# A segment attention kernel on one core: GpSimd's fills issued a segment later, the fourth segment's owners computed one step sooner, another PSUM bank for the last prefix, and one table's work placed behind a row's scaling

## The chip, the cores and the metric

The kernel runs on one core of a Trainium2 chip. The metric is the device time of one execution in microseconds (us); the number given for a kernel is the median of several executions. The engines are written as in the profile: PE is TensorE, DVE is VectorE, ACT is ScalarE, POOL is GpSimd, SP is SyncE, which here only starts transfers. PEld is the weight load of PE.

## The reference

16384 tokens with 256 features each carry a segment number from 0 to 7. Attention runs inside each segment, and a column normalisation over all tokens follows. The segment numbers are not sorted, so that `searchsorted` gives a start for each segment, and a token's position is its distance to that start; positions outside 0 to 3071 wrap or are dropped by the scatter. The part that matters:

```python
q = feat @ Wq; k = feat @ Wk; v = feat @ Wv              # 256 -> 32, 32, 256
starts = jnp.searchsorted(bids, jnp.arange(B, dtype=bids.dtype))
pos = jnp.arange(N, dtype=bids.dtype) - starts[bids]
pad = lambda x: jnp.zeros((B, LMAX, x.shape[-1]), x.dtype).at[bids, pos].set(x)
mask = jnp.zeros((B, LMAX), bool).at[bids, pos].set(True)
scores = jnp.einsum('bld,bmd->blm', pad(q), pad(k))
attn = jax.nn.softmax(jnp.where(mask[:, None, :], scores, NEG), axis=-1)
t = jnp.einsum('blm,bmd->bld', attn, pad(v))[bids, pos] @ Wt
tn = (t - t.mean(0)) / jnp.sqrt(t.var(0) + EPS) * gamma + beta
return feat + jax.nn.relu(tn)
```

## The kernel before, in words

Every engine has its own instruction stream, and the order inside a stream is the order in which the Python code emits the operations. `pg.op` records what each operation reads and writes, and puts a semaphore wait in front of it wherever it needs something of another engine. So a line that is moved in the Python code is moved in its engine's queue, with everything that it issues, and an operation that has to wait holds back all that stands behind it on its engine.

**Stages.** A setup reads the segment numbers, searches the starts, and prepares segments 0 and 1. Then a loop over segments e = 0 to 6 works in steps u = 0 to 5, written (e,u) here. In it segment e is attended, segment n = e+1 is projected and scored, and the rows of segment e+2 are listed and gathered. Segment 7 and the normalisation follow, with the stores of all rows.

**A segment** has up to six tiles of 128 rows; tiles 4 and 5 are guarded by a run-time count (`present`), and segments 0 and 1 have four tiles with this input. A conditional operation passes its semaphore to the next unconditional one of its engine.

**Listing.** For each segment, DVE's `owners(e)` (seven operations) marks the tokens that own a slot and ends with a running count in `lm[:, e]`. `prefix(lo, hi, bank)` adds the counts over partitions with two small PE products into a PSUM bank; DVE reads it as `cbeg`, `n_bc` and `n_1`. `list_tests` makes two comparison masks `ge` of 128x768 on DVE (fp16 in, bf16 out, line 835), `list_half(e, h, bank)` multiplies them on PE (six products) and its `finish` turns the result into row numbers `idx` on DVE (`lr`, `junk`, `jc`, `idx`) and issues three gathers `xs<-in_r_feat,idx` on POOL.

**Attending.** `attend(e,u)` is a row of products `ps<-vs,pa` on PE into bank 4 or 5 by the parity of u. `attended(e,u)` takes a reciprocal `rdens` on DVE (line 859) and scales the row on ACT into `tk` (line 817). Only then may attend(e,u+2) write the bank again. `xt_main` and `xt_rest` transpose gathered rows into `xT`, `project` makes q and k (`k` is copied by DVE, `q` by ACT), `scores` makes `pa`, `values` makes `vs`.

**PSUM banks.** Banks 0 to 3 are `ps_s`, 4 and 5 `ps_o`, 6 and 7 `ps_m`. `nb()` hands out banks 6 and 7 in turn to `xt_main`, `xt_rest`, `project` and `values`.

**Fillers.** `everyone()` and `tables()` are lists of small DVE jobs for all segments at once. `slot()` takes the next one off the list `work`; the table `steps` says at which steps of e = 0 to 3 one is taken. In e = 0 the jobs of u = 1 to 5 are a, b, `third`, c, d; in e = 1 those of u = 0, 1, 2, 4, 5 are f, g, h, g2, and the first of `tables()` (`frow`, `gbase`, `w`). `third` handles segment 3: `owners(3)`, its prefix and its `list_tests`. Job g is the prefix of segments 4 to 8, h makes `reads` from `br_f`, g2 reads the table `turn_of`.

**Fills.** POOL sets several tensors to constants: `acc` (the sums of the normalisation, 128x512), `xl` and `tl` (128x768), `ridl`, `ecat` (128x512) and sixteen single elements of `turn_of`. `moments` adds into `acc` on DVE from (1,1) on.

Of the kernel before, what the change touches and what calls it, by code (L numbers as in the profile page):

```python
# [899 lines left out]
def fast_path(nc, feat, bids, wq, wk, wv, wt, gamma, beta, out, bad):  # L900
# [231 lines left out]
    pg.set("POOL", ones_n[:], 1.0 / N)  # L1132
    pg.set("POOL", rdens[:], 1.0)
    pg.set("POOL", graw[:], 0.0)
    for i in range(4):
        s = slice(32 * i, 32 * i + NB)
        pg.dma("SP", graw[s, 0, :], gamma.rearrange("(c i) -> c i", i=32))
        pg.dma("SP", graw[s, 1, :], beta.rearrange("(c i) -> c i", i=32))
# [311 lines left out]
    xt_rest(0, sB)  # L1450
    h1()
    last_()
    pg.set("POOL", acc[:], 0.0)
    pg.set("POOL", xl[:], 0.0)
    pg.set("POOL", tl[:], 0.0)
    pg.set("POOL", ridl[:], NB * FW)
    pg.set("POOL", ecat[:], 0.0)
    for i, g in enumerate(ORDER):
        pg.set("POOL", turn_of[:, g : g + 1], float(i + 1))
    values(0, 0, bank[1])  # L1460
    scores(0, 0, range(4))
    project(0, 1, ps_m[0])
# [22 lines left out]
    def everyone():  # L1485
# [24 lines left out]
            pg.scan(lm[:, NB, 0:J], ones[:], lose[:])  # L1510

        def g():
            for go in prefix(4, NL, ps_s[3]):
                go()

        def g2():
# [161 lines left out]
    reads_at = {(NB - 4, 2 + t): (NB - 2, (t,)) for t in range(4)}  # L1678
    reads_at.update({(NB - 3, t): (NB - 2, (3 + t,)) for t in (1, 2)})
    reads_at.update({(NB - 3, 3 + t): (NB - 1, (2 * t, 2 * t + 1)) for t in range(3)})  # L1680
    lag, ready = [], []
    steps = {0: (1, 2, 3, 4, 5), 1: (0, 1, 2, 4, 5), 2: (0, 2, 3, 5), 3: (0, 1, 2, 3, 5)}
    def third():
        owners(3)
        first, then, last_ = prefix(3, 4, ps_s[3])
        first()
        then()
        last_()
        list_tests(3, FT)
# [3 lines left out]
    for e in range(NB - 1):  # L1693
# [11 lines left out]
        for u in range(FT):  # L1705
            if ahead <= NB and u == 0 and e:
                first = list_half(ahead, 0, ps_s[2])
            attend(e, u)
            if e == 0 and u == 0:
                second_list()  # L1710
                attended(e, u)
                first = list_half(ahead, 0, ps_s[2])
            if ahead <= NB and u == 0:
                first()
                if LTs == FT:
                    second = list_half(ahead, 1, ps_s[3])
            slot(int(u in steps.get(e, range(FT))))
            if u == 4 and e + 3 <= NB and e:
                list_tests(e + 3, FT if e + 3 < NB else LT)
            if u == 4:  # L1720
                values(n, 0)
            if u == 5:
                values(n, 1)
            if e == NB - 2 and u == 3:
                group_in(1)
            if (e, u) != (0, 0):
                opened = attended(e, u)
            if u == 0:
                if ahead <= NB and LTs == FT:
                    second()  # L1730
                if ahead == NB:
                    others()
                xt_main(n, 0)
                xt_main(n, 1)
            if u == 1:
                xt_rest(n)
                project(n, 0)
                scores(e, 1, None)
            if u == 3:
                project(n, 1)  # L1740
                scores(n, 0, range(4))
            if u == 4:
                scores(n, 0, range(4, 6))
            if u == 5:
                values(n, 2)
            for x in ready:
                moments(*x)
            ready = []
            lag.append((e, u))
            for _ in range(0 if e == 0 else 2 if u % 2 else 1):  # L1750
                if lag:
                    square(*lag[0])
                    ready.append(lag.pop(0))
            if e == 0 and u == 1:
                pg.tr32(gb[:].rearrange("p s i -> p (s i)"), graw[:].rearrange("p s i -> p (s i)"))
                for e_ in range(3, NB):
                    pg.dma(
                        "SP", xs[:, e_ * FT : (e_ + 1) * FT, :], zt[:].unsqueeze(1).to_broadcast([P, FT, D]), [opened]
                    )
            if e == 0 and u in (1, 5):  # L1760
                pg.copy("ACT", spot[:], ones[:, 0:1])
            if (e, u) in reads_at:
                gather_reads(*reads_at[e, u], opened)
            if e == NB - 2 and u == 1:
                group_in(0)
            if e == NB - 2 and u > 3:
                group_in(u - 2)
            if e == NB - 2 and u == 5:
                group_in(4)
            if e == 4 and u == 3:  # L1770
                pg.set("POOL", tk[:, TT - 2 : TT, :], 0.0)
                pg.register("POOL", "writes", writes[:], 16 * (6 * NB + LT), 16 * (4 * NB + LT - 1))
                pg.register("POOL", "lastg", lastg[:], NG, 1)
                pg.register("POOL", "third", third_l[:], 1)
                for e_ in range(NB):
                    pg.register("POOL", ("g", e_), upto[0:1, e_ : e_ + 1], NG, 1)
                    pg.register("POOL", e_, tiles_i[0:1, e_ : e_ + 1], 2)
# [238 lines left out]
```

## Time and profile before

| | |
|---|---|
| time, median of 3 runs | 312.52 us (310.84 to 314.01) |
| the profiled execution's own time | 313.69 us |
| its span, first to last instruction | 311.4 us |
| PE busy | 252.2 us, 81% |
| DVE busy | 229.3 us, 74% |
| ACT busy | 135.8 us, 44% |
| POOL busy | 129.7 us, 42% |
| mean granted TensorE clock | 0.906 |

A row of the timeline gives the start in us, the duration, the engine and line, the operation with what it writes and reads, how many were merged, and in brackets how long the engine stood idle before it and what ended that. A row of the stage view gives a stretch of time, its length, each engine's busy time, the granted clock (1.00 is full, 0.50 half), the share of the DMA engines and GB/s. Lines such as L807 or L835 are those of helpers, so that groups are told apart by the names of the tiles.

### The profile page before, as it was taken

The numbers are of one execution on the slowest core, as the hardware profiler recorded it, in microseconds if no ns is written. First come the engines' busy times: TensorE is split into PE (matmuls) and PEld (weight loads), VectorE is DVE, ScalarE is ACT, GpSimd is POOL, SyncE is SP. The second block draws the span as 40 slices with busy tenths as digits, with TensorE's granted clock in tenths as the row PEclk, the third lists the DMA queues.
The fourth block names the chain that finished last, engine by engine and source line by source line (L and its number), as shares of the span: only waits on it lengthen the run. The fifth ranks groups of instructions, "written<-read, shape, count | busy, mean of one in ns | idle before, by whom it ended". The sixth has DMA issues, their size and how long they took to land.

```text
span 311.4 us, 4481 instructions
## 1 busy us (share of the span) xinstructions
PE 252.2 (81%) x1194; PEld 166.8 (54%) x1194; DVE 229.3 (74%) x718; ACT 135.8 (44%) x292; POOL 129.7 (42%) x155
## 2 busy tenths in 40 slices
PE   1779689899799898999999999989977786573820
PEld 1656555766575677687878778757523221121200
DVE  7866788779999896736664765767389999999600
ACT  7346234258474628644754583564421121211110
POOL 3436580340350071006312853742212347778674
PEclk9989796999999999999999999999998579859575
DMA  3102069422122021112021320579999999999984
GB/s 98 35 24 67 3 203 346 157 82 69 52 84 71 34 70 29 67 61 80 27 95 36 90 94 24 196 259 378 339 364 408 349 421 413 402 419 393 424 358 177
DMA packets 23240, 56.82 MB, mean 182 GB/s; under 512 B 4768, under 2 KB 15858, under 8 KB 19114
## 3 DMA queue, kind: packets, MB, share of 16 engines
q1 hardware_dynamic: 17434, 45.77, 39.2%
q0 software_dynamic: 5232, 10.18, 10.2%
q10 hardware_dynamic: 544, 0.52, 0.5%
q8 instruction: 13, 0.21, 0.3%
q14 instruction: 17, 0.14, 0.1%
HBM read 26.73 MB, written 28.61 MB: 178 GB/s over the span
## 4 chain that ended last, share of the span: by engine, by line
PE 39%; DVE 30%; DMA 14%; ACT 7%; issue 6%; POOL 2%; DVEq 1%; SPq 0%; POOLq 0%; ACTq 0%
PE ps L807 37%; DMA out<-f 14%; DVE acc L846 4%; DVE f L826 3%; DVE w L826 2%; DVE junk L833 2%; PE ps L812 2%; DVE k L823 2%; DVE tk L826 2%; POOL out L892 2%; ACT pa L817 1%; DVE ge L835 1%; ACT xT L817 1%; ACT tk L817 1%; DVE both L851 1%
## 5 line engine op out<-in xcount | busy, mean ns | idle before, releaser
L882 POOL DMA_INDIRECT xs<-in_r_feat,idx x48 | 51.0, 1063 | 101.2 <-DVE idx L846 77.1
L807 PE MATMUL ps<-vs,pa 128*128 128x257 f32 x312 | 73.6, 384 | 4.7 <-ACT sq L817 3.6
L807 PEld LDWEIGHTS ps<-vs,pa 128*128 128x128 f32 x312 | 57.1, 189 | 16.5 <-ACT sq L817 4.8
L807 PE MATMUL ps<-f,ident 128*128 128x512 f32 x52 | 38.3, 855 | 19.6 <-DMA f<-in_r_feat 14.4
L892 POOL DMA_INDIRECT out<-tk,idx x39 | 42.9, 1100 | 26.8 <-DVE tk L826 10.4
L817 ACT ACTIVATE tk<-ps,rdens 128x256 f32<-128x256 f32 x46 | 22.2, 483 | 61.8 <-DVE rdens L859 61.8
L807 PE MATMUL ps<-wvt,xT 128*128 128x256 f32 x156 | 39.6, 405 | 0.3 <-ACT pa L817 0.3
L822 ACT COPY f<-ps 128x512 f32<-128x512 f32 x26 | 13.9, 590 | 58.9 <-PE ps L807 58.9
L807 PEld LDWEIGHTS ps<-wvt,xT 128*128 128x128 f32 x156 | 30.9, 202 | 11.0 <-issue 4.3
L807 PEld LDWEIGHTS ps<-f,ident 128*128 128x128 f32 x52 | 11.7, 259 | 36.5 <-DMA f<-in_r_feat 19.3
L846 DVE SCALAR_TENSOR_TENSOR acc<-sq,reads_r,acc 128x256 f32<-128x256 f32 x45 | 21.6, 480 | 8.8 <-ACT sq L817 8.8
L817 ACT ACTIVATE pa<-ps,mask 128x512 f32<-128x512 f32 x39 | 24.0, 690 | 7.5 <-PE ps L807 7.4
L826 DVE TENSOR_TENSOR tk<-tk,ps 128x1024 f32<-128x1024 f32 (+1 forms) x30 | 24.2, 843 | 0.3
L882 POOL DMA_INDIRECT reads_r<-reads_of,idx x12 | 13.4, 1120 | 24.8 <-ACT sq L817 11.8
L826 DVE TENSOR_TENSOR f<-f,ps 128x512 f32<-128x512 f32 x38 | 23.3, 681 | 0.6 <-PE ps L807 0.6
L807 PE MATMUL ps<-q,k 32*128 32x512 f32 (+2 forms) x154 | 21.2, 486 | 1.5 <-ACT pa L817 1.1
L846 DVE SCALAR_TENSOR_TENSOR acc<-tk,reads_r,acc 128x256 f32<-128x256 f32 x45 | 21.5, 478 | 1.2 <-ACT tk L817 0.7
L807 PE MATMUL ps<-xT,w 128*128 128x512 f32 (+1 forms) x60 | 20.5, 474 | 0.5 <-ACT xT L817 0.4
L823 DVE COPY k<-ps 32x128 f32<-32x128 f32 x40 | 11.8, 294 | 12.0 <-PE ps L807 11.1
L807 PE MATMUL ps<-vs,pb 128*128 128x257 f32 x82 | 19.6, 387 | 0.0
L807 PEld LDWEIGHTS ps<-vs,pb 128*128 128x128 f32 x82 | 15.0, 189 | 6.5 <-issue 2.3
L817 ACT ACTIVATE q<-ps,cqk 96x512 f32<-96x512 f32 (+3 forms) x24 | 14.6, 608 | 7.3 <-PE ps L807 7.0
(260 smaller groups left out, 357.1 us busy)
## 6 DMA issues: line engine op xcount, KB each, us to landing
f<-in_r_feat SPq DMA_DIRECT2D x16, 1024.0 KB, 12.8
out<-f SPq DMA_DIRECT2D x16, 1024.0 KB, 15.8
t_rows<-tk SPq DMA_DIRECT2D x8, 512.0 KB, 3.9
xs<-zt SPq DMA_DIRECT2D x5, 768.0 KB, 10.3
t_rows<-tk SPq DMA_DIRECT2D x8, 256.0 KB, 2.2
eb<-edge_of SPq DMA_DIRECT2D x16, 96.0 KB, 2.3
xs<-in_r_feat,idx POOLq DMA_INDIRECT x48, 2.8
out<-tk,idx POOLq DMA_INDIRECT x39, 7.2
```

The lines of the kernel that those rows point to most:

```text
L807: "PE", lambda e: e.matmul(out, lhsT, rhs, start=start, stop=stop, skip_group_check=True),
L812: return self.op("PE", lambda e: e.transpose(out, in_, ident), [in_, ident], [out])
L817: "ACT", lambda e: e.activation(out, in_, func, bias=bias, scale=scale), [in_, *more], [out]
L822: return self.op("ACT", lambda e: e.copy(out, in_), [in_], [out])
L823: return self.op(eng, lambda e: e.tensor_copy(out, in_), [in_], [out])
L826: return self.op(eng, lambda e: e.tensor_tensor(out, a, b, op), [a, b], [out])
L833: lambda e: e.tensor_scalar(out, a, s1, s2, op0, op1, accum_out=accum)
L835: else e.tensor_scalar(out, a, s1, s2, op0, op1),
L846: else e.scalar_tensor_tensor(out, a, s, b, op0, op1),
L851: return self.op("DVE", lambda e: e.tensor_reduce(out, in_, AX.X, op), [in_], [out])
L882: lambda e: e.indirect_dma_start(out=out, out_offset=None, in_=table, in_offset=bass.IndirectOffsetOnAxis(ap=ind, axis=0), bounds_check=n ...
L892: lambda e: e.indirect_dma_start(out=table, out_offset=bass.IndirectOffsetOnAxis(ap=ind, axis=0), in_=src, in_offset=None, bounds_check=n ...
```

## The change

Five edits. The fill of `acc` goes from the end of the setup to its beginning. The other fills go into `later_sets`, which is called at the end of (1,0). `owners(3)` leaves `third` and is emitted in (0,0), behind `attended(0,0)` and ahead of the list of segment 2. The prefix of segments 4 to 8 takes its bank from `nb()` instead of bank 3. At (1,5) the slot is taken behind `attended` instead of ahead of it.

```diff
     pg.set("POOL", graw[:], 0.0)
+    pg.set("POOL", acc[:], 0.0)
...
-    pg.set("POOL", acc[:], 0.0)
-    pg.set("POOL", xl[:], 0.0)
-    pg.set("POOL", tl[:], 0.0)
-    pg.set("POOL", ridl[:], NB * FW)
-    pg.set("POOL", ecat[:], 0.0)
-    for i, g in enumerate(ORDER):
-        pg.set("POOL", turn_of[:, g : g + 1], float(i + 1))
+
+    def later_sets():
+        pg.set("POOL", xl[:], 0.0)
+        pg.set("POOL", tl[:], 0.0)
+        pg.set("POOL", ridl[:], NB * FW)
+        pg.set("POOL", ecat[:], 0.0)
+        for i, g in enumerate(ORDER):
+            pg.set("POOL", turn_of[:, g : g + 1], float(i + 1))
+
...
-            for go in prefix(4, NL, ps_s[3]):
+            for go in prefix(4, NL):
...
+    LATE = ((1, 5),)
...
     def third():
-        owners(3)
         first, then, last_ = prefix(3, 4, ps_s[3])
...
                 second_list()
                 attended(e, u)
+                owners(3)
                 first = list_half(ahead, 0, ps_s[2])
...
-            slot(int(u in steps.get(e, range(FT))))
+            if (e, u) not in LATE:
+                slot(int(u in steps.get(e, range(FT))))
...
                 opened = attended(e, u)
+            if (e, u) in LATE:
+                slot()
...
+            if e == 1 and u == 0:
+                later_sets()
```

In POOL's stream, from the last fill of the setup on, the difference is this; the first twelve gathers are those of segments 0 and 1, and the next six of each segment follow.

```order
 L865 MEMSET rdens 128x48
 L865 MEMSET graw 128x64
-L882 DMA xs<-in_r_feat,idx 128x256 x12
 L865 MEMSET acc 128x512
+L882 DMA xs<-in_r_feat,idx 128x256 x24
 L865 MEMSET xl 128x768
 L865 MEMSET tl 128x768
```

The fill of `acc` now stands ahead of all gathers, and the other fills stand behind the gathers of segments 2 and 3. The next piece is DVE's stream before, at (0,1) to (0,3): `k1` is the copy of project(1,0), the reciprocal of `ps4` is that of (0,2), then come the seven operations of `owners(3)` and the first reading of its prefix.

```order
L823 COPY k1_68<-ps6 32x128 x4
L862 STREAM_TRANSPOSE gb_140<-graw_180 128x64
L826 TENSOR_TENSOR w3_183<-m3_182,st_bc_194 128x1024
L859 RECIPROCAL rdens_119<-ps4 128x1
L835 TENSOR_SCALAR own1_170<-b_f_185 128x128
L846 SCALAR_TENSOR_TENSOR own1_170<-tok_187,st_lo_195,own1_170 128x128
L846 SCALAR_TENSOR_TENSOR own1_170<-tok_187,st_hi_196,own1_170 128x128
L846 SCALAR_TENSOR_TENSOR lose_190<-tok_187,st_bc_194,same_188 128x128
L826 TENSOR_TENSOR lose_190<-lose_190,own1_170 128x128
L826 TENSOR_TENSOR own1_170<-own1_170,lose_190 128x128
L855 SCALAR_TENSOR_TENSOR lm_52<-ones_86,own1_170 128x128
L823 COPY cbeg_107<-ps3 128x1
```

And this is DVE's stream of the changed kernel at (0,0); the reciprocal of `ps4` is now that of (0,0), and `lr` begins the list of segment 2.

```order
L859 RECIPROCAL rdens_119<-ps4 128x1
L835 TENSOR_SCALAR own1_170<-b_f_185 128x128
L846 SCALAR_TENSOR_TENSOR own1_170<-tok_187,st_lo_195,own1_170 128x128
L846 SCALAR_TENSOR_TENSOR own1_170<-tok_187,st_hi_196,own1_170 128x128
L846 SCALAR_TENSOR_TENSOR lose_190<-tok_187,st_bc_194,same_188 128x128
L826 TENSOR_TENSOR lose_190<-lose_190,own1_170 128x128
L826 TENSOR_TENSOR own1_170<-own1_170,lose_190 128x128
L855 SCALAR_TENSOR_TENSOR lm_52<-ones_86,own1_170 128x128
L826 TENSOR_TENSOR lr_121<-rcol_106,ps2 128x3
```

The seven operations stand ahead of the whole list of segment 2 and of the reciprocal of (0,1), and `cbeg` of segment 3 follows the reciprocal of (0,2) directly. The third place is PE's stream at (1,1): before, the prefix of segments 4 to 8 (`lm` with `tri` and `onesb`), the conditional transposes of xt_rest(2) and project(2,0) (`w4`) stood so:

```order
L807 MATMUL ps3<-lm_52,tri_163 128x5
L807 MATMUL ps3<-lm_52,onesb_164 128x5
L772 COMPARE_AND_BRANCH
L812 MATMUL ps7<-ident_85,xs_49 128x128 x2
L772 UNCONDITIONAL_BRANCH
L807 MATMUL ps6<-xT_62,w4_63 128x512 x2
```

In the changed kernel the same operations write other banks:

```order
L807 MATMUL ps7<-lm_52,tri_163 128x5
L807 MATMUL ps7<-lm_52,onesb_164 128x5
L772 COMPARE_AND_BRANCH
L812 MATMUL ps6<-ident_85,xs_49 128x128 x2
L772 UNCONDITIONAL_BRANCH
L807 MATMUL ps7<-xT_62,w4_63 128x512 x2
```

The prefix goes from bank 3 to bank 7, xt_rest(2) from bank 7 to 6, and project(2,0) into the bank that holds the prefix; banks 6 and 7 are exchanged in all that follows.

## The prediction

> **What bounds the kernel now.** I read three views: the busy time by stage, to find where which engine is full; the timeline of the stages that the diff touches, for what each engine waits for; and the granted clock in those stretches. The stages first.
>
> ```profile
> 32.60:62.57 29.97, 24.01 (x110) 18.11 (x110) 24.49 (x103) 10.69 (x22) 12.66 (x30) 0.83 0.59 185
> 65.19:84.05 18.86, 16.34 (x86) 11.73 (x85) 17.91 (x66) 11.19 (x25) 2.63 (x4) 1.00 0.20 63
> ...
> 120.00:190.00 70.00, 69.14 (x379) 53.62 (x378) 42.48 (x143) 41.59 (x100) 23.07 (x21) 1.00 0.20 64
> ...
> 230.00:311.40 81.40, 47.16 (x174) 15.78 (x174) 62.21 (x93) 13.87 (x26) 47.87 (x44) 0.73 0.93 373
> ```
>
> The columns are PE, PEld, DVE, ACT, POOL, clock, DMA share and GB/s. From 120 us on PE is full (69.1 of 70 us), and at the end the DMA engines are (0.93). Neither stage is touched. Both are fed by engine queues that run in order, so a saving before 84 us should arrive at the end nearly whole. From 65 to 84 us DVE is full (17.9 of 18.9 us). From 32.6 to 62.6 us, where (0,0) to (1,0) lie, nobody is full: DVE works 24.5 of 30 us, PE 24.0, and the clock is down to 0.83. That stage holds the first three edits. Its waits:
>
> ```profile
> 33.07 1.60 DVE L835 TENSOR_SCALAR ge<-it,cbeg 128x768 bf16<-128x768 f16 x1
> ...
> 34.60 0.76 DVE L835 TENSOR_SCALAR ge<-it,cend 128x768 bf16<-128x768 f16 x1
> ...
> 40.49 0.16 DVE L859 RECIPROCAL rdens<-ps 128x1 f32<-128x1 f32 x1
> ...
> 41.85 1.22 DVE L823 COPY k<-ps 32x128 f32<-32x128 f32 x4 [1.19 <-PE ps L807]
> ...
> 46.94 0.18 PE L807 MATMUL ps<-lm,tri 128*128 128x1 bf16 x1 [1.65 <-DVE lm L855]
> ...
> 47.18 0.16 DVE L823 COPY cbeg<-ps 128x1 f32<-128x1 f32 x1 [0.30 <-PE ps L807]
> ...
> 48.08 0.40 DVE L835 TENSOR_SCALAR ge<-it,cbeg 128x768 bf16<-128x768 f16 x1
> ...
> 54.24 0.17 DVE L859 RECIPROCAL rdens<-ps 128x1 f32<-128x1 f32 x1 [0.84 <-PE ps L807]
> ...
> 56.40 0.16 DVE L826 TENSOR_TENSOR lr<-rcol,ps 128x3 f32<-128x3 f32 x1 [1.99 <-PE ps L807]
> ...
> 62.41 0.16 DVE L846 SCALAR_TENSOR_TENSOR idx<-ps,jc 128x3 int32<-128x3 f32 x1
> ```
>
> DVE and PE hold each other up in turn. The two `ge` of segment 2 take from 33.07 to 35.36, 2.3 us; the same pair costs about 0.8 us at 48.08, so 1.5 us are lost. Later DVE stands idle for PE for 1.19 + 0.30 + 0.84 + 1.99 = 4.3 us, and in between PE stands 1.65 us for the last operation of `owners(3)`.
>
> **Edit 1, the fills.** What lies beside the slow `ge`, and what does not mind a fill:
>
> ```profile
> 33.01 0.75 POOL L865 MEMSET xl<- 128x768 f32 x1
> ...
> 34.40 0.73 POOL L865 MEMSET ecat<- 128x512 f32 x1
> ...
> 1.70 0.79 DVE L823 CAST lm<-pcol 128x9 bf16<-128x9 f32 x1
> ...
> 156.87 0.54 POOL L865 MEMSET tk<- 128x512 f32 x1
> ...
> 156.89 0.48 DVE L846 SCALAR_TENSOR_TENSOR acc<-tk,reads_r,acc 128x256 f32<-128x256 f32 x1
> ```
>
> The large fills run from 33.01 to 35.13 without a gap, and the `ge` end right behind. So a DVE operation with one input from SBUF is held while POOL fills; a small cast at 1.70, 0.79 us long beside POOL's setup, shows the same. The two-input sum at 156.89 ran beside a fill in 0.48 us and was not held. Moving the fills away gives DVE and PE back 1.5 us.
>
> The Trainium skill, "GPSIMD Engine Reference", section "8. Key points", says that POOL shares its SBUF interfaces with DVE and contends with instructions in a 2-port mode or with two SBUF inputs. The first half agrees with the `ge` (1.60 us), the second half not with the sum at 156.89 (0.48 us); what it would make of this change is a rival below.
>
> **Edit 2, `owners(3)`.** Its seven operations keep their cost and move ahead of the list of segment 2:
>
> ```profile
> 44.53 0.21 DVE L835 TENSOR_SCALAR own<-b_f 128x128 f32<-128x128 f32 x1
> ...
> 46.45 0.43 DVE L855 TENSOR_TENSOR_SCAN lm<-ones,own 128x128 bf16<-128x128 f32 x1
> ...
> 41.64 3.64 PE L807 MATMUL ps<-vs,pa 128*128 128x257 f32 x16
> ...
> DMA to landing us min/median/max: 2.9/6.3/7.1
> ```
>
> They take 44.53 to 46.88, 2.35 us. Queued behind them are the list, its gathers, and the reciprocal of (0,1), on which ACT and then attend(0,3) wait. That reciprocal comes at 40.49 - 1.5 + 2.35 = 41.3. PE is 1.5 us early at project(1,0), so the `k` copies follow at once, at 41.5, and the 1.19 us go. Attend(0,3) may start when ACT has scaled the row, at about 42.0, and takes half of 3.64: 43.8. The prefix of segment 3 then needs nothing more, since `lm` was ready at 37; DVE reaches `cbeg` at 44.2 (41.5 + 2.6 for `k`, `gb`, `w`, as from 41.85 to 44.44) and finds it. That is 3.0 us ahead of 47.18: 1.5 + 1.19 + 0.30. The gathers of segment 2 start 0.8 us later. The fourth of them, issued at about 43.9 and at worst 7.1 us on its way (the landing row is for these six gathers), is there at 51, and xt_main(2) asks for it at 52.5: covered, with 1.5 us to spare.
>
> **The clock.** Whether the 0.84 + 1.99 us go as well depends on PE's pace:
>
> ```profile
> 44.89:48.30 3.41, 1.42 (x11) 0.71 (x10) 2.91 (x15) 0.23 (x1) 1.48 (x2) 1.00 1.05 345
> 48.30:51.71 3.41, 3.41 (x10) 1.79 (x6) 3.38 (x11) 2.39 (x5) 0.00 (x0) 0.50 1.10 340
> ...
> 78.99:82.40 3.41, 1.68 (x14) 1.48 (x15) 3.27 (x15) 1.57 (x4) 0.00 (x0) 1.00 0.23 77
> ...
> 24.96 1.89 PE L807 MATMUL ps<-wvt,xT 128*128 128x256 f32 x8
> ...
> 49.56 6.45 PE L807 MATMUL ps<-wvt,xT 128*128 128x256 f32 x16
> ```
>
> A stretch in which PE worked 1.42 of 3.41 us, the one with the wait for `lm`, is followed by one at half clock; one with 1.68 of 3.41 kept full clock (at 82.4 it went on at 1.00). The sixteen products of `values` took 6.45 us where 2 x 1.89 = 3.8 would do, and the scores before them lost about 0.7 us: 3.4 us for the cold clock. Without the wait, PE goes from the scores at 44.4 to the list of segment 3 in 8.4 - 3.4 = 5.0 us, and has it by 49.9. DVE gets there at 53.4 - 3.0 = 50.4. So both idle times go, but with half a microsecond to spare. DVE then works without a gap, and the `idx` row at 62.41 comes 1.5 + 4.3 = **5.8 us** earlier.
>
> **Edit 3, the bank.**
>
> ```profile
> 61.40 1.26 ACT L817 ACTIVATE xT<-ps,negx 128x512 f32<-128x512 f32 x2
> ...
> 62.63 0.18 PE L807 MATMUL ps<-lm,tri 128*128 128x5 bf16 x1 [1.50 <-DVE idx L846]
> ...
> 63.16 1.99 PE L807 MATMUL ps<-xT,w 128*128 128x512 f32 x4
> ...
> 63.65 0.15 DVE L835 TENSOR_SCALAR n<-ps 128x5 f32<-128x5 f32 x1
> ...
> 65.19 1.27 DVE L823 COPY k<-ps 32x128 f32<-32x128 f32 x4 [1.00 <-PE ps L807]
> ```
>
> PE no longer waits for `idx` to free bank 3, but bank 7 has its own readers. The prefix waits for the first `xT`, xt_rest(2) for the second (62.66), and project(2,0), which now writes the prefix's bank, for DVE's last reading of it, `n` at 63.80. DVE reads the prefix 0.3 us earlier, so `n` would end at 63.5 where project started at 63.16: a wait of 1.50 us turns into one behind it, and `k` comes 0.4 us later. Bounds: a gain of 0.3 if the reading is not waited for, a loss of 0.9 if nothing is read earlier and a semaphore's delay is added. I take a loss of **0.4**, which the rows give.
>
> **The fills in their new place.**
>
> ```profile
> 65.97 1.00 POOL L882 DMA_INDIRECT xs<-in_r_feat,idx  x1 [0.30 <-issue]
> ...
> 67.29 0.22 DVE L823 CAST br_f<-br_i 128x128 f32<-128x128 int32 x1
> ...
> 2.98 0.14 POOL L865 MEMSET graw<- 128x64 f32 x1
> ...
> 3.18 0.28 DVE L835 TENSOR_SCALAR sa<-irow,pcol 128x128 f32<-128x128 f32 x1
> ```
>
> They start when the last gather of segment 3 has been issued, 66.97 on this clock (both sides shift alike, DVE by 0.4 less), and run for 2.1 us. The DVE is full there. Of its operations then, the sums and the readings of `reads` have two inputs, the reciprocals read PSUM, and one, the cast `br_f`, has one SBUF input. It would start at 67.7 on this clock and be held to the end of `tl` at 68.3: **0.6** lost, between 0 and the 1.5 of the `ge`. The table `turn_of` is done by then plus 0.7 us, well before job g2. In the setup the fill of `acc` starts at 3.1, beside `sa`, on DVE's chain of the first list: **0.3** lost (0 to 0.54, the length of a fill of 128x512).
>
> **Edit 5, (1,5).**
>
> ```profile
> 79.21 0.16 DVE L859 RECIPROCAL rdens<-ps 128x1 f32<-128x1 f32 x1
> ...
> 80.72 1.14 PE L807 MATMUL ps<-vs,pa 128*128 128x257 f32 x4 [1.92 <-ACT sq L817]
> ...
> 84.24 0.47 ACT L817 ACTIVATE tk<-ps,rdens 128x256 f32<-128x256 f32 x1 [3.27 <-DVE rdens L859]
> ```
>
> The reciprocal moves ahead of 1.5 us of table work, so ACT's `vs` and PE's rest of attend(2,0) at 80.72 come 1.5 us earlier. But DVE is full, its sum is the same, and the next row's scaling at 84.24 still waits 3.27 us for DVE. What hides the gain is DVE's work up to the reciprocal of (2,0). Bounds 0 to 1.5; I take **0**, as that last row says.
>
> **Sum.** 5.8 - 0.4 - 0.6 - 0.3 = 4.5 us. The profiled execution took 313.69 us (span 311.4 and 2.3 around it), so 309.2. That execution is 1.2 us above the median of the runs, 312.52, and I guess that part of this is cold stretches of just the kind that go; half of it taken off gives **308.6**.
>
> **Rivals.**
>
> *A, the clock stays cold.* The spare 0.5 us is thin. If the scores and `values` of segment 1 still run at half clock, DVE keeps its 0.84 + 1.99: 5.8 - 2.8 - 1.3 = 1.7 gained, 311 to 312. For it: once cold, the stretch from 48.30, worked to the full, did not bring the clock back at once, and the sixteen products took 6.45 us. Against: the stretch with the long wait is gone.
>
> *B, two-input operations are held too.* Then all of DVE's work beside the fills waits 2.1 us instead of the cast's 0.6: 1.5 less gained, 310 to 310.7. Against it stands the sum at 156.89, for it only that this is a single row. This is the second half of the rule of the Trainium skill's "GPSIMD Engine Reference" named above. The same time would come out if the `ge` were slow for a reason other than the fills (the change not doing what it says): 1.5 less gained.
>
> *C, slower: the cold clock moves.* With DVE ahead and project(2,0) waiting for DVE, PE has 2.4 us between the end of attend(1,1) and project(2,0), with 0.6 us of work in them. A stretch of 3.41 us around it holds about 1.6 us of work, between the 1.42 that was followed by half clock and the 1.68 that was not. If it is followed by two cold stretches, it costs the 3.4 us worked out above; together with A: 1.7 gained, 3.4 lost, 315.4 from the profiled time, 314 to 315.4. It decides from the point where the busy part falls below half.
>
> **How the numbers follow.** Forecast 0.52 (307 to 309.8); A 0.15; B with the change that doesn't do what it says 0.18; C 0.10; a larger gain, no collision of the fills and something from (1,5), 0.05 (below 307). The range 306.6 to 312.2 takes in the forecast, A and B, and the loss bounds of edit 3, the cast and the setup together (2.9 us lost of 5.8: 310.8); it leaves C and the tails out. A measurement of this kernel can tell about 1%, 3.1 us: below 309.4 is faster. That is most of the forecast, a quarter of B and the larger gain: 0.55. Above 315.6 lies a third of C and what I did not see: 0.05. The rest, 0.40, is within 1%.
>
> **What would show it.** The two `ge` of segment 2 at 0.4 us each; no wait of PE for `lm` at (0,3); granted clock 1.00 from there to the list of segment 3; `idx` of segment 3 at 56 to 57 us; project(2,0) waiting for DVE's `n`; the cast `br_f` at 0.8 us beside a fill, the sums at 0.48. I am wrong if half-clock stretches turn up again before 62 us, if a sum grows beside a fill, or if the saving at 62 us is no longer there at 120 us.

## The result, and the profile after

The changed kernel takes **309.3 us** (median of 21 runs, 306.66 to 311.57), the kernel before 312.52 us (21 runs beside them). The ratio is 0.990, interval 0.988 to 0.993; a second, later measurement gave 0.990 (0.987 to 0.994), where 0.994 or more was to mean that the first was partly chance. The forecast was 308.6 us. All ratios here leave out executions more than 1.5% above the fastest of their kernel, and where executions spread widely this moves them (10 of the 35 of the kernel before go on the chip of the first four experiments), so the plain medians stand beside them. The profiled execution of after took 307.41 us, 6.3 us less than that of before, twice the gain of the medians; where the surplus comes from is the first reading. The stages in the profile of after, with the same columns as before:

```profile
30.87:56.11 25.24, 20.37 (x112) 15.01 (x112) 22.89 (x104) 10.30 (x22) 10.60 (x10) 1.00 0.64 204
60.35:79.22 18.87, 17.97 (x90) 12.69 (x89) 17.76 (x65) 10.95 (x24) 3.74 (x22) 0.98 0.16 52
115.00:185.00 70.00, 69.15 (x379) 53.63 (x378) 42.78 (x144) 41.56 (x100) 23.02 (x21) 1.00 0.20 64
223.50:304.97 81.47, 46.69 (x176) 15.43 (x174) 64.02 (x97) 13.86 (x26) 46.64 (x44) 0.72 0.95 382
```

The first row answers to 32.60:62.57 of before. The stage from the prefix of segment 2 to the list of segment 3 shrank from 30.0 to 25.2 us, DVE now works 22.9 of them and the clock is 1.00 all through it. The middle of the program is as full as it was.

The stage also starts 1.7 us earlier, at 30.9 instead of 32.6 us. In the second profile of the same kernel it starts at 33.3 us, and in those of the experiments anywhere from 31.2 to 34.4 us. So this is chance and not the change. Another 1.7 us lie behind the column statistics, where half-clock stretches come and go: 87.1 us before, 85.4 after, 86.8 in the second profile of after. For every kernel below I therefore count from DVE's first reading of the prefix of segment 2, `cbeg` at 32.61 us before and 30.88 after. Three milestones are used: the end of the list of segment 3 (its last `idx`), the first `k` of project(2,0), and the first `k` of project(3,0).

| counted from the prefix of segment 2, us | list of segment 3 | `k` of segment 2 | `k` of segment 3 |
|---|---|---|---|
| before | 29.96 | 32.58 | 55.34 |
| after, first profile | 25.23 | 29.47 | 52.40 |
| after, second profile | 25.05 | 28.87 | 52.21 |

From `k` of segment 3 to the column statistics (DVE's `st_t`, which reads the sums) before and after need the same time, 136.3 us. So the list gains 4.7 to 4.9 us, and 2.9 to 3.1 us of it come through, beside the 3.2 us of the medians. The waits of DVE and PE in the gaining stage, from the timeline of after:

```profile
31.34 0.55 DVE L835 TENSOR_SCALAR ge<-it,cbeg 128x768 bf16<-128x768 f16 x1
31.81 0.40 DVE L835 TENSOR_SCALAR ge<-it,cend 128x768 bf16<-128x768 f16 x1
...
39.60 0.16 DVE L859 RECIPROCAL rdens<-ps 128x1 f32<-128x1 f32 x1
39.79 1.27 DVE L823 COPY k<-ps 32x128 f32<-32x128 f32 x4
...
42.16 0.17 PE L807 MATMUL ps<-lm,tri 128*128 128x1 bf16 x1
...
42.52 0.14 DVE L823 COPY cbeg<-ps 128x1 f32<-128x1 f32 x1
...
48.66 0.16 DVE L859 RECIPROCAL rdens<-ps 128x1 f32<-128x1 f32 x1
49.94 0.16 DVE L826 TENSOR_TENSOR lr<-rcol,ps 128x3 f32<-128x3 f32 x1 [1.12 <-issue]
...
55.95 0.16 DVE L846 SCALAR_TENSOR_TENSOR idx<-ps,jc 128x3 int32<-128x3 f32 x1
```

Three of the four idle times of DVE are gone (before `k`, `cbeg` and `rdens`), and PE no longer waits for `lm`. The fourth, 1.99 us before `lr`, did not go: 1.12 us are left, and what ends them is no other engine but "issue". Behind the list stands the second loss, PE and DVE around the last prefix, with the clock of the stretches there:

```profile
55.67 0.18 PE L807 MATMUL ps<-lm,tri 128*128 128x5 bf16 x1 [2.02 <-ACT xT L817]
...
57.00 3.31 PE L807 MATMUL ps<-xT,w 128*128 128x512 f32 x4 [0.25 <-DVE n L835]
...
60.35 1.27 DVE L823 COPY k<-ps 32x128 f32<-32x128 f32 x4 [2.99 <-PE ps L807]
...
54.10:57.51 3.41, 1.13 (x5) 0.61 (x6) 2.98 (x22) 2.05 (x5) 2.47 (x3) 1.00 1.03 331
57.51:60.92 3.41, 3.41 (x6) 1.69 (x5) 0.54 (x2) 1.77 (x4) 2.80 (x4) 0.50 0.35 116
```

PE works 1.13 of 3.41 us, the next stretch runs at half clock, and project(2,0) takes 3.31 us instead of 1.99. Before, the half-clock stretches of this part lay at 34.6 to 38.1 and 48.3 to 55.1 us; now there is one, and it lies where DVE has nothing else to do. The prediction named a half-clock stretch ahead of 62 us as a sign that it is wrong, and this is one; it lies behind the list and not ahead of it.

### The profile page after: what moved, and what is told of

It reads as the page before. It is cut to its first block, busy times and chain, and to the rows that moved or that the text cites. A ratio compares the mean times of both kernels' runs of the same rounds, so it can differ in the third digit from the quotient of the medians.

```text
span 305.0 us, 4482 instructions
## 1 busy us (share of the span) xinstructions
PE 246.9 (81%) x1194; PEld 163.1 (53%) x1194; DVE 228.0 (75%) x718; ACT 135.4 (44%) x292; POOL 128.1 (42%) x155
## 4 chain that ended last, share of the span: by engine, by line
PE 35%; DVE 32%; DMA 14%; issue 7%; ACT 7%; POOL 1%; DVEq 1%; POOLq 0%; SPq 0%; ACTq 0%
PE ps L807 34%; DMA out<-f 14%; DVE acc L846 4%; DVE junk L833 3%; DVE f L826 3%; DVE w L826 2%; DVE tk L826 2%; POOL out L892 1%; ACT pa L817 1%; DVE k L823 1%; PE ps L812 1%; DVE ge L835 1%; ACT xT L817 1%; ACT tk L817 1%; DVE both L851 1%
## 5 line engine op out<-in xcount | busy, mean ns | idle before, releaser
L892 POOL DMA_INDIRECT out<-tk,idx x39 | 41.7, 1069 | 27.9 <-DVE tk L826 11.9
L807 PE MATMUL ps<-f,ident 128*128 128x512 f32 x52 | 37.5, 836 | 18.2 <-DMA f<-in_r_feat 12.4
L807 PE MATMUL ps<-wvt,xT 128*128 128x256 f32 x156 | 37.1, 384 | 0.5 <-DVE acc L846 0.3
L807 PEld LDWEIGHTS ps<-wvt,xT 128*128 128x128 f32 x156 | 28.9, 190 | 10.0 <-issue 3.5
L817 ACT ACTIVATE sq<-tk 128x256 f32<-128x256 f32 x42 | 17.3, 429 | 0.3
```

Of the source, the lines that this page charges most:

```text
L807: "PE", lambda e: e.matmul(out, lhsT, rhs, start=start, stop=stop, skip_group_check=True),
L817: "ACT", lambda e: e.activation(out, in_, func, bias=bias, scale=scale), [in_, *more], [out]
L892: lambda e: e.indirect_dma_start(out=table, out_offset=bass.IndirectOffsetOnAxis(ap=ind, axis=0), in_=src, in_offset=None, bounds_check=n ...
```

## The experiments

The medians of the same kernel before differ from chip to chip (311.6 to 315.5 us), and single executions spread by some 1.3 us to each side. A ratio here is good to 0.3 to 0.6%, so the milestones of the profiles, one profile for each row, carry most of the verdicts. All of them:

| kernel | list | `k` of segment 2 | `k` of segment 3 | ratio to before (95%) | median (before beside it) |
|---|---|---|---|---|---|
| edit 1 alone (fills) | 27.04 | 29.65 | 53.38 | 0.999 (0.996 to 1.003) | 313.06 (313.41) |
| edit 2 alone (owners) | 26.57 | 29.18 | 51.94 | 0.995 (0.992 to 0.999) | 311.95 (313.41) |
| after, last prefix on bank 3 | 25.07 | 27.69 | 51.42 | 0.997 (0.993 to 1.001) | 310.99 (313.41) |
| the same again | 25.09 | 28.94 | 51.95 | 0.999 (0.994 to 1.003) | 314.36 (315.51) |
| after, PE kept busy | 25.13 | 28.86 | 51.97 | 0.998 (0.994 to 1.002) | 312.17 (313.41) |
| after without edit 5 | 25.21 | 29.55 | 52.36 | 0.992 (0.989 to 0.996) | 309.19 (311.63) |
| after, register read earlier | 24.18 | 28.62 | 51.37 | 0.984 (0.980 to 0.989) | 307.84 (312.22) |
| after, row (1,0) early | 25.21 | 25.31 | 49.87 | 0.983 (0.977 to 0.989) | 308.50 (312.22) |
| both | 24.27 | 24.59 | 48.87 | 0.981 (0.976 to 0.985) | 306.47 (311.63) |
| both, fills later still | 24.26 | 24.58 | 48.64 | 0.981 (0.978 to 0.985) | 306.51 (312.22) |
| the same, row (2,0) early | 24.25 | 24.57 | 48.19 | 0.986 (0.981 to 0.991) | 307.52 (311.63) |

**Edit 1 alone**: `acc` in the setup, the other fills behind (1,0).

```diff
     pg.set("POOL", graw[:], 0.0)
+    pg.set("POOL", acc[:], 0.0)
...
-    pg.set("POOL", acc[:], 0.0)
-    pg.set("POOL", xl[:], 0.0)
...
+            if e == 1 and u == 0:
+                later_sets()
```

> Edit 1 alone: the fills moved, all else as before. Theory (the stage from 33 to 62 us is a chain that passes between DVE and PE, and each edit pays only for its own wait): the two ge of segment 2 fall from 2.3 to about 0.9 us, but the wait of PE for owners(3) and the half-clock stretches behind it stay, so 1.3 us are gained, ratio 0.996; in the profile PE still waits over 1 us for lm at (0,3). Rival (the fills are the whole gain): ratio 0.990, 3 us. Second rival (the fills were not what held the ge): ratio 1.000, ge still over 1 us.

Both `ge` took 0.41 us, so the fills did slow them. PE still waited 1.65 us for `lm`, as forecast. The list gained 2.9 us, more than the 1.3 of the theory: the half-clock stretch behind that wait was shorter this time, and the sixteen products of `values` took 5.08 us instead of 6.45. `k` of segment 3 gained only 2.0 us, and the ratio shows nothing (0.3 us faster, between 1.4 faster and 0.9 slower). Where the 1.0 us between list and `k` of segment 3 goes stands in the timeline:

```profile
33.45 0.41 DVE L835 TENSOR_SCALAR ge<-it,cbeg 128x768 bf16<-128x768 f16 x1
...
46.09 0.18 PE L807 MATMUL ps<-lm,tri 128*128 128x1 bf16 x1 [1.65 <-DVE lm L855]
...
64.42 0.76 POOL L865 MEMSET xl<- 128x768 f32 x1
...
64.75 1.20 DVE L823 CAST br_f<-br_i 128x128 f32<-128x128 int32 x1
```

The cast `br_f`, 0.22 us long before, begins beside the fills and takes 1.20 us. Another 1.5 us are lost behind `k` of segment 3 in this profile; the experiments with bank 3 come back to that.

**Edit 2 alone**: `owners(3)` moved from `third` to (0,0).

```diff
     def third():
-        owners(3)
...
                 attended(e, u)
+                owners(3)
```

> Edit 2 alone: owners(3) in (0,0), fills, bank and order as before. Theory: the ge of segment 2 still take 2.3 us, PE's wait for lm at (0,3) is gone, and with it the half-clock stretches from there to the list of segment 3; about 2 us gained, ratio 0.9935. Rival (a mere reordering of DVE work, the gain comes from the fills): ratio 0.999 to 1.001, with DVE's idle time before the list of segment 3 as long as before.

```profile
33.02 1.60 DVE L835 TENSOR_SCALAR ge<-it,cbeg 128x768 bf16<-128x768 f16 x1
...
45.24 0.17 PE L807 MATMUL ps<-lm,tri 128*128 128x1 bf16 x1
```

The list gained 3.4 us although `ge` still took 1.60 us, PE no longer waited for `lm`, and `k` of segment 3 came as early as with all five edits. By the milestones the owners alone bring what the change brings; the ratio, with 1.5 us (0.3 to 2.6), shows half of it. This profile has no half-clock stretch between 38 and 229 us, and project(2,0) took its 1.98 us.

**The last prefix on bank 3 again**, everything else as after:

```diff
-            for go in prefix(4, NL):
+            for go in prefix(4, NL, ps_s[3]):
```

> The changed kernel with edit 3 undone: the prefix of segments 4 to 8 goes to bank 3 again. Theory (the bank only exchanges one wait for another, 0.3 us): 0.3 us faster than the changed kernel, ratio to before 0.989, and a half-clock stretch at project(2,0) is as likely as with the bank. Rival (the bank's wait is what lets the clock fall at project(2,0)): 1.6 us faster than the changed kernel, ratio 0.985, project(2,0) in 2.0 us at full clock.

In the first profile project(2,0) ran at full clock, `k` followed the list by 2.62 us as before the change, and `k` of segment 3 came at 51.42; yet by the ratio the kernel is only 1.0 us faster than before (0.4 slower to 2.3 faster; the plain medians say 2.4). A loss behind the list was in sight: `br_f` again took 1.20 us. As the two readings spoke against each other, the kernel was run a second time:

> The changed kernel with the last prefix on bank 3 again, a second time, since the first profile and the first times of it speak against each other. If the bank's edit costs what the profiles show (the first `k` of segment 3 at 51.42 us behind the prefix of segment 2 without it, 52.40 and 52.21 with it), this kernel has the half-clock stretch at the projection of (2,0) in no profile, `k` of segment 3 at 51.2 to 51.8 us, and a median of 0.986 to 0.990 of the kernel before. If the first times are right, the bank's edit gains: 0.994 to 0.999, and then the loss stands behind 84 us. If both were chance, 0.990 to 0.994, and the edit is worth nothing that can be measured.

```profile
59.91 3.23 PE L807 MATMUL ps<-xT,w 128*128 128x512 f32 x4
...
173.03 0.69 ACT L817 ACTIVATE xT<-ps,negx 128x512 f32<-128x512 f32 x1 [1.52 <-remote]
```

The half-clock stretch now stands at project(2,0) with bank 3 too, so the bank's edit does not cause it; where it falls varies from run to run. The ratio was again no better than 0.994 at the low end (the plain medians give 0.996). Both runs lose behind 84 us: from `k` of segment 3 to the column statistics they took 137.3 and 139.0 us, where before and after took 136.3, here with a wait of ACT's `xT` at 173 us for something that the view calls remote; no row shows what it is. Two things could make these 1.0 to 2.7 us. One is the exchange of banks 6 and 7 behind the prefix; but before, with bank 3, does not have them. The other is the chip, since both runs were on other chips than the second measurement of after. The three other kernels that ran on the chip of the first took 137.1 to 137.8 us for the same stretch, one of them with the banks of after (the next experiment). But that one loses its 1.1 us only at the end of the stretch, where ACT waits longer for the DMA of `ecat`. Up to the product of `acc` with `ones_n` it needs 132.3 us from `k` of segment 3, as before and after do (132.2), while the four profiles with bank 3 on these two chips (edits 1 and 2 alone keep it as well) need 133.0 to 134.9, and they alone have such remote waits of ACT. Nor would a loss that a chip brings to every kernel show in a ratio taken on that chip; of the kernel before there is no profile from these chips. So neither explanation fits all of it, and whether the bank's edit gains or loses in the end stays **open**.

**PE kept busy**: 14 products of 128x128 without use in front of the last prefix.

```diff
+            if (e, u) == (1, 1):
+                for _ in range(14):
+                    pg.mm(ps_s[0][:, 0:P], ident[:], ones[:])
```

> The changed kernel with fourteen extra products of 128x128 on PE between attend(1,1) and the prefix of segments 4 to 8; their result is not used. They take about 1.8 us of the 2.0 us in which PE stands idle there. Theory (that idle time lets the clock fall, and the half-clock stretch makes project(2,0) 1.3 us longer): project(2,0) takes 2.0 us at granted clock 1.00, and the time falls by about 1 us against the changed kernel, ratio to before 0.987. Rival (the half clock there was chance, or does not reach the end): same as the changed kernel or up to 0.3 us slower, ratio 0.990 to 0.991.

```profile
61.10 1.99 PE L807 MATMUL ps<-xT,w 128*128 128x512 f32 x4 [0.74 <-issue]
...
56.07:59.48 3.41, 3.41 (x29) 3.30 (x29) 3.18 (x16) 1.64 (x4) 2.80 (x3) 1.00 1.06 335
59.48:62.90 3.42, 2.67 (x14) 1.49 (x13) 1.17 (x9) 1.41 (x4) 2.17 (x4) 1.00 0.60 197
...
221.37 0.42 ACT L817 ACTIVATE ecat<-ecat 128x256 f32<-128x256 f32 x1 [2.54 <-DMA ecat<-t_rows,eidx]
```

With PE at work the clock stayed at 1.00 and project(2,0) took 1.99 us, which is what the theory says of PE's idle time. One profile alone does not show it, since the first one with bank 3 kept full clock without such products; the kernels with the early row, below, bear it out. The products cost most of what they saved: they ran to 59.9 us, and DVE had to wait 0.73 us for the prefix behind them. The forecast of the time failed: the ratio is 0.998 (0.994 to 1.002), not 0.987. Of that the profile shows 1.1 us, behind the longer wait for `ecat` in the last row (2.54 us for 0.50 in after); the rest is not explained.

**After without edit 5**: at (1,5) the slot stands ahead of `attended` again.

```diff
-    LATE = ((1, 5),)
+    LATE = ()
```

> The changed kernel without its last part: the job beside row (1,5) stands ahead of that row's scaling again, as before. Theory of the forecast (this part is worth 0): TensorE waits longer for (2,0) at about 74 us, some 1.5 to 1.9 us instead of 0.47, but no longer at the rest of segment 3's transposes (0.2 instead of 1.64 us), and the first `k` of segment 3 comes 52.0 to 52.6 us behind the prefix of segment 2, as after the change (52.40 and 52.21 in two profiles). Rival: this part carries some of the gain, and `k` of segment 3 comes at 53.2 us or more; the median then rises by 1 us or more over the changed kernel's.

```profile
76.30 1.14 PE L807 MATMUL ps<-vs,pa 128*128 128x257 f32 x4 [1.93 <-ACT sq L817]
...
81.01 0.63 PE L812 MATMUL ps<-ident,xs 128*128 128x128 f32 x4 [0.18 <-ACT xT L817]
```

In after the same two rows read so:

```profile
74.60 1.14 PE L807 MATMUL ps<-vs,pa 128*128 128x257 f32 x4 [0.47 <-ACT sq L817]
...
80.77 0.63 PE L812 MATMUL ps<-ident,xs 128*128 128x128 f32 x4 [1.64 <-ACT xT L817]
```

PE waits 1.93 + 0.18 us without the edit and 0.47 + 1.64 us with it, 2.11 us both times. `k` of segment 3 comes at 52.36 instead of 52.40 or 52.21. The edit moves a wait and is worth nothing that shows.

**The register read earlier.** At the start of segment 1's rows (e = 1) DVE's sequencer reads the number of tiles of segment 2 into a register. This kernel lets it do so in job c, behind the long reduction that makes `pos`.

```diff
         def c():
             by_token(pos[:], w3[:])
+            pg.register("DVE", 2, tiles_i[0:1, 2:3], 2)
...
-        for eng in ("PE", "ACT", "DVE"):
+        for eng in ("PE", "ACT", "DVE") if e != 1 else ("PE", "ACT"):
```

> The changed kernel with one more edit: VectorE reads its register with segment 2's number of tiles inside the job that computes `pos`, instead of at the start of segment 1's rows. Theory (the missing term of the forecast): in the trace after, `lr` at 49.94 us stands 1.12 us behind the end of the instruction before it, because VectorE's sequencer reads the register there; before the change this read lay inside the 1.99 us wait at the same place. So the 1.12 us go to at most 0.1, the list of segment 3 ends 1.1 us earlier counted from the prefix of segment 2, and the first `k` of segment 2 comes 28.4 us behind that prefix (29.47 after the change). Rival: ScalarE, whose `xT` the prefix of the last segment waits for (2.02 us), is late next: the idle goes, the list ends earlier, but `k` stays at 29.3 to 29.5. Median: 0.9865 to 0.987 of the kernel before by the theory, 0.990 by the rival.

The group of DVE's register reads in after, the single read at this place in after and in the kernel before, and two timeline rows of this kernel:

```profile
L688 DVEq TENSOR_LOAD <-tiles_i x8: 303/315/989, 20.7 to 187.5; - x8
...
L688 DVEq TENSOR_LOAD <-tiles_i x1: 989/989/989, 48.6 to 48.6; - x1
...
L688 DVEq TENSOR_LOAD <-tiles_i x1: 1019/1019/1019, 54.3 to 54.3; - x1
...
49.36 0.16 DVE L859 RECIPROCAL rdens<-ps 128x1 f32<-128x1 f32 x1
49.59 0.16 DVE L826 TENSOR_TENSOR lr<-rcol,ps 128x3 f32<-128x3 f32 x1
```

One of the eight reads of after takes 989 ns (the columns are minimum, median, maximum in ns, then first and last start in us), and it starts at 48.6 us, in the idle time before `lr`. Before, the same read took 1019 ns from 54.3 us on, inside the wait of 1.99 us: the trace of the kernel before already showed it. With the read behind the reduction, `lr` follows `rdens` at once, and the list ends 0.9 to 1.05 us earlier. So this was the 1.12 us. `k` of segment 3 gains 0.8 to 1.0 us: the theory, not the rival, though `k` of segment 2 at 28.62 missed its 28.4, since a half-clock stretch at 57.0 made project(2,0) 3.51 us long.

**Row (1,0) early**: its scaling goes ahead of job f (`o` and two scans, 3 us of DVE), and jobs g and h one step later each.

```diff
-    LATE = ((1, 5),)
+    LATE = ((1, 0), (1, 5))
...
-    steps = {0: (1, 2, 3, 4, 5), 1: (0, 1, 2, 4, 5), 2: (0, 2, 3, 5), 3: (0, 1, 2, 3, 5)}
+    steps = {0: (1, 2, 3, 4, 5), 1: (0, 2, 3, 4, 5), 2: (0, 2, 3, 5), 3: (0, 1, 2, 3, 5)}
```

> The changed kernel with the job of the list's ranks moved behind the scaling of row (1,0), by the means the change uses for row (1,5), and the next job one step later. Theory: TensorE's idle of 2.02 us before the prefix of the last segment and of 3.31 us before the projection of (2,0) come from ScalarE and VectorE being late with row (1,0); with the scaling of that row ahead of the job, ScalarE's `xT` comes about 1 to 2 us earlier, TensorE's idle before the prefix falls under 0.5 us, no half-clock stretch follows at 57 to 61 us, and the projection of (2,0) takes under 2.1 us per piece sequence as at full clock. The first `k` of segment 2 comes 26.5 to 28.0 us behind the prefix of segment 2 (29.47 after the change); median 0.981 to 0.986 of the kernel before. Rival: the list is the bound and is only put off by the row's scaling, so that the idle stands somewhere else: `k` at 29.2 to 30.5, median 0.990 to 0.994.

```profile
54.02 1.88 PE L807 MATMUL ps<-xT,w 128*128 128x512 f32 x4
...
56.56 1.27 DVE L823 COPY k<-ps 32x128 f32<-32x128 f32 x4
...
58.39 0.18 PE L807 MATMUL ps<-lm,tri 128*128 128x5 bf16 x1 [0.75 <-ACT q L817]
...
58.76 0.16 DVE L823 COPY cbeg<-ps 128x5 f32<-128x5 f32 x1
```

The list ends when it did (25.21), but `k` of segment 2 follows it after 0.1 us instead of 4.2, PE's idle times and the half clock at project(2,0) are gone. The ratio gives 5.3 us (3.6 to 7.1) over before, but it rests on four of only six executions (304.05 to 310.11 us, with the profiled one at 304.09); the plain medians differ by 3.7 us. `k` came earlier than the theory had it, 25.31 for 26.5 to 28.0. About 1.4 us is given back up to `k` of segment 3: the readings of the last prefix (1.3 us of DVE, from 56.03 to 57.36 in after, while DVE had to wait anyway) now stand behind `k`, where DVE is full.

**Both together**, with and without fills one segment later still (`xl`, `tl`, `ridl`, `ecat` behind (2,0), while `turn_of` stays):

```diff
             if e == 1 and u == 0:
+                turn_sets()
+            if e == 2 and u == 0:
                 later_sets()
```

> The two edits of the two other kernels together, and the fills of `xl`, `tl`, `ridl` and `ecat` one segment later still (only `turn_of` stays). Theory: the 1.1 us of the register and the 1.5 to 3 us of the early row add up, and `br_f`, which takes 0.22 us alone and 1.20 us beside a fill, stays at 0.22: first `k` of segment 2 at 25.4 to 27 us behind the prefix of segment 2, first `k` of segment 3 as much earlier, median 0.976 to 0.983 of the kernel before. Rival: the two do not add up, because both shorten the same wait; `k` no earlier than in the better of the two, median within 0.002 of it.

> The register's early read and the early row (1,0) together, with all fills where the change has them. Theory: the fills are worth little where they stand; only `br_f` and casts beside them are held, so the first `k` of segment 2 comes at 24.4 to 24.8 us behind the prefix of segment 2 as with the fills a segment later (24.58), and the first `k` of segment 3 at 48.6 to 49.6 us (48.64 there), the difference being at most the 1.0 us by which `br_f` is held. Rival: the last 1.2 us between the early row alone (49.87) and all three edits (48.64) came from the fills and not from the register: `k` of segment 3 at 49.8 us or more.

The two edits add up (48.87 from 49.87 and 51.37). The fills' third place is worth 0.2 us in the profile and nothing in the medians: 306.47 and 306.51 us. By their medians these are the fastest of all kernels here, 1.9% (1.5 to 2.4) faster than before.

**Row (2,0) early too**:

```diff
-    LATE = ((1, 0), (1, 5))
+    LATE = ((1, 0), (1, 5), (2, 0))
```

> The three edits together, and the scaling of row (2,0) ahead of its job too. Theory: the reciprocal of (2,0) moves ahead of two products of 128 by 1024 elements (2.45 us), ScalarE's `xT` behind it comes earlier, TensorE's wait of 1.64 us before the rest of segment 3's transposes falls under 0.3 us, and the first `k` of segment 3 comes 1.2 to 1.6 us earlier: 47.0 to 47.5 us behind the prefix of segment 2 (48.64 without this edit); median 0.975 to 0.979 of the kernel before. Rival: the list of segment 4, which these two products belong to, is next to the bound, and row (2,1) waits for it instead: `k` of segment 3 no earlier than 48.3 us.

```profile
77.23 0.60 PE L812 MATMUL ps<-ident,xs 128*128 128x128 f32 x4
...
80.90 0.16 DVE L859 RECIPROCAL rdens<-ps 128x1 f32<-128x1 f32 x1
81.09 1.27 DVE L823 COPY k<-ps 32x128 f32<-32x128 f32 x4
...
89.60:93.00 3.40, 1.38 (x7) 0.87 (x5) 3.31 (x9) 1.74 (x4) 0.00 (x0) 1.00 0.11 35
93.00:96.40 3.40, 3.10 (x5) 1.49 (x6) 2.42 (x10) 3.40 (x8) 0.00 (x0) 0.51 0.36 121
```

PE's wait of 1.64 us went, as the theory says, but DVE reaches `k` without a pause only at 81.09: the gain is 0.45 us of 1.2 to 1.6, and the rival has the mechanism (its bound was 48.3, measured 48.19). PE then idles more and a half-clock stretch follows at 93 us; from `k` of segment 3 to the column statistics this profile takes 137.9 us, 1.2 more than without this edit. The medians, 307.5 to 306.5 us of six executions each, do not separate the two kernels.

## Why the prediction was right, and where its terms were off

**Where the time comes from: right.** The two `ge` gave 1.4 us for the 1.5 forecast. The seven operations of `owners(3)` took 33.04 to 35.39, the 2.35 us forecast, and what stands behind them came where the rows said. Counted from the prefix, the reciprocal of (0,1) was forecast at 8.7, `k` at 8.9 and `cbeg` at 11.6 us; they came at 8.7, 8.9 and 11.6. PE kept full clock up to the list of segment 3, so rival A is out. The half microsecond that PE was to have in hand at that list was not there: its six products ended at 48.89 us, when DVE had just come to 48.82.

**The idle time before `lr`: the step that failed.** I took all 1.99 us as a wait for PE, because PE ended it. In that wait lay a register read of DVE's sequencer (1.02 us from 54.3 us on), which PE's lateness had hidden; with PE early, it came out as 1.12 us. The 5.8 us of the list became 4.7, and the experiment with the earlier read brings 0.9 to 1.05 us back.

**The bank: right in size.** From the last `idx` to project(2,0) went 0.59 us before and 0.89 after: 0.3 us for the 0.4 forecast, with the wait for `n` that was named; with bank 3 again it was 0.59 and 0.58. That is this place alone; what the exchange of banks does behind 84 us is not settled.

**The clock at project(2,0): underrated.** Rival C described it and put it at 0.10, as a loss of 3.4 us in two stretches. It came as one stretch in both profiles of after, and project(2,0) took 3.31 and 2.89 us for 1.99: **1.3 and 0.9 us**. Five of the seven profiles with edits 1 and 2 and without the early row have it (after twice, bank 3 the second time, without edit 5, the register). It belonged into the sum, not into a rival. Of the other two, one has the filler products, and one (bank 3, the first time) kept full clock without them. With the filler products or the early row, five profiles in all, PE has no idle time above 0.74 us ahead of project(2,0), and none of them has the half clock there: so PE's idle time brings it about, though not every time, and the early row shows that this idle time is due to DVE's order.

**The fills in their new place: right in mechanism, 0 for 0.6.** From the timeline of after, POOL and DVE at (1,1), and the setup:

```profile
60.50 0.75 POOL L865 MEMSET xl<- 128x768 f32 x1
61.18 0.75 POOL L865 MEMSET tl<- 128x768 f32 x1
...
61.89 0.54 POOL L865 MEMSET ecat<- 128x512 f32 x1
...
61.65 0.48 DVE L846 SCALAR_TENSOR_TENSOR acc<-tk,reads_r,acc 128x256 f32<-128x256 f32 x1
62.05 0.48 DVE L846 SCALAR_TENSOR_TENSOR acc<-sq,reads_r,acc 128x256 f32<-128x256 f32 x1
62.45 0.22 DVE L823 CAST br_f<-br_i 128x128 f32<-128x128 int32 x1
...
3.06 0.51 POOL L865 MEMSET acc<- 128x512 f32 x1
...
3.18 0.48 DVE L835 TENSOR_SCALAR sa<-irow,pcol 128x128 f32<-128x128 f32 x1
```

Because `k` came late, the cast began when the large fills were over, and was not held. In the other profiles with the fills at this place it took 0.22 to 1.20 us, so the 0.6 was the middle of what can happen, and 0 was luck. What the cast loses comes through: from `k` of segment 2 to that of segment 3 it takes 22.76 us before, and 23.01, 23.11, 23.73 and 23.73 where the cast was held by 0.24, 0.36, 0.98 and 0.98 us (bank 3 the second time, PE kept busy, edit 1 alone, bank 3 the first time). Something else is lost there too in both profiles of after: 22.93 us with nothing held, and 23.34 with 0.28. The setup's `sa` took 0.48 instead of 0.28 us: 0.2 lost for 0.3. The two sums beside fills took 0.48 us, so rival B is refuted, and with it, for these sums beside fills, the half of the rule of the Trainium skill, "GPSIMD Engine Reference", section "8. Key points", that names instructions with two SBUF inputs. The half that the one-input operations bear out (`ge`, 1.60 us beside fills and 0.41 without) is what edit 1 rests on.

**Edit 5: right**, 0 us: the wait only moved.

**The sum: near in part by luck.** Counted from the prefix of segment 2, the 5.8 us of the list became 4.7 (register). Less 0.3 (bank) and 1.3 (clock), 3.1 us are left at `k` of segment 2, and 2.9 at `k` of segment 3; where the 0.2 between goes is not shown. The forecast for this place was 4.8 (5.8 - 0.4 - 0.6). The setup's 0.2 us lie ahead of the prefix, where chance moves the start by more than that, so nothing here shows whether they come through. So the gain was forecast some 1.9 us too large: 1.1 for the register, 1.3 for the clock and the 0.2, less 0.7 that bank and cast did not cost. Three things hid most of that: the step from the profiled execution to the median, half of 1.2 us by a guess, was too small by the other half (0.6); 0.3 was taken off for the setup; and the medians gained 3.2 us, 0.3 more than this profile's milestones show. So 308.6 came within 0.7 us of 309.3.

## What to carry to other kernels

An idle time that another engine ends can hide a second cause: before booking it as gained, list what the waiting engine's own sequencer does in it (here a register read of 1 us). A gain on the engine that makes the lists is worth only what the next consumer can take; 4.7 us became 2.9, for the most part because PE then stood idle and fell to half clock, and a change of the order, with the row's scaling ahead of 3 us of list work, brought more (2.5 us at `k` of segment 3) than the fills and the bank together. Where a short operation may or may not fall beside a fill, give it as a range, since a shift of half a microsecond elsewhere decides it.

## What the runs showed of the hardware

- A read of a value from memory into a register of DVE's sequencer took 0.30 to 1.02 us; behind an operation of 1.9 us it cost nothing, in front of a ready one 1.1 us.
- A cast with one input from SBUF was held up to 1.0 us beside POOL's fills of 0.5 to 0.8 us each (1.20 us for 0.22); sums with two inputs were not (0.48 us).
- The granted clock changed in steps of about 3.41 us in these profiles. Stretches with PE busy for 1.07 to 1.71 us of that were followed by half clock, others with 1.67, 1.68, 1.88 and 2.36 us were not; one with 2.07 us was. These busy times do not fix a border. The Trainium skill, "TensorE: Matmul & The Clock Gate", section "Why this matters for your kernels", asks for no idle gaps of TensorE above some 3 us; in after one of 2.02 us was enough, with shorter ones beside it.
- The kernel before has medians of 311.6, 312.2, 313.4 and 315.5 us on four chips, which differ by more than the whole effect of the change. Only ratios taken on one chip say anything here.
